# Selective scans: another order of the three VectorE operations of a step, the sliced copy on another engine, and the delta product in four row groups

## The chip, the cores and the metric

The kernel runs on one core of a Trainium2 chip. The metric is the device time of one execution in microseconds (us). Engines are named as the profile names them: PE is TensorE, DVE is VectorE, ACT is ScalarE, POOL is GpSimd, SP is the engine that only issues transfers.

## The reference, cut to what matters

Two layers run on x of shape (4, 64, 64, 128): four images of L = 4096 tokens with 128 channels. Layer 0 is a Mamba block with three scan orders (forward, backward, and "sliced": the tokens taken in 16 interleaved slices). Layer 1 is attention with 16 heads of 8 channels, a small feed-forward part, and a mixture of 64 experts. The change touches layer 0 alone:

```python
xz = in_proj_w @ groupnorm(x)             # 2 * 256 rows: x and z
# for each of three orders:
x = silu(causal_conv1d(x, conv_w, conv_b))          # 4 taps
dt_raw, Bm, Cm = split(x_proj_w @ x, [8, 16, 16])   # along rows
delta = softplus(dt_w @ dt_raw + dt_b)              # 256 rows from 8
A = -exp(A_log)                                     # 256 x 16
def step(h, u_, de_, b_, c_):                       # over 4096 tokens
    dA = exp(de_[..., None] * A)
    h = h * dA + (de_ * u_)[..., None] * b_[:, None, :]
    return h, einsum('bdn,bn->bd', h, c_)
y = (selective_scan(x, delta, A, Bm, Cm) + D * x) * silu(z)
```

The sum of the three orders' y goes through out_proj_w and is added to x.

## The kernel before, in words

Everything is float32. A sequence of 4096 tokens is cut into NC = 4 chunks of T = 1024.

`Inputs` makes what the scans need. `norm` (L251) brings an image, transposes it and normalizes it to the tile xn (128 channels x 4096). `slices` (L301) makes xs, the same tokens in the sliced order, by one GpSimd copy (L305). `of_chunk` makes one chunk of one order: the convolution folded into the input projection (matmuls L361, cv), silu on ACT (L368), the x projection (L375, xd) and its copy to SBUF (L378, xds), whose rows hold B, C and the 8 rows of dt_raw. From these 8 rows the matmuls L394 make the two halves of delta's argument (dt, 2 halves of 256 channels x 2 cuts of 512 tokens). Softplus is made from ACT passes (L399 to L410) and three matmuls a piece that add the parts (L417, sp); VectorE finishes r = delta (L422) and delta * u (L426). delta, du, u, B and C go to DRAM by POOL's queue. The tile pool `ps` has three PSUM tiles.

`Scans.of_image` does an image's scans: 3 orders x 4 chunks x 32 steps = 384 steps. In a step the 128 partitions are 16 channels x 8 states, over 1024 tokens. Its parts:

- `load(s)`, two steps ahead: for every second step delta and du are spread from DRAM over the states (512 KB each), delta by SP's queue, du by SP's, or for image 0 by ACT's; for every fourth step u; at the start of a chunk B and C.
- `exp(s)` (L501), one step ahead on ACT: dA.
- `step(s)` on VectorE: the product du * B (L510), the scan h (L513, tensor_tensor_scan), the product h * C (L515). On GpSimd the last column of h is kept as the start of the next chunk (L514, ends).
- `total(s)` (L521) on TensorE: the sum over the states into one PSUM bank y for a group of four steps. The sums of a group's steps j = 0 and 1 are issued five and four steps later than these, those of j = 2 and 3 four and three steps later.
- `out` (L537) on VectorE: y + D * u, stored by POOL's queue. Then the bank is free.

Buffers: for even steps the product with B goes to a new tile dB (three of them); for odd steps it overwrites du (four). The product with C overwrites the product with B, and the sums L521 read it there. dA has two tiles, delta three, h two.

The order of the work is written out by hand: each part is a generator, and `Pace` advances generators by given shares. There are these stages. The *fill* (to about 2360 us in the profile) advances image 0's scans once for every 1.5 advances of the inputs of all four images, two pieces of inputs at a time. Then `opening(0)` prepares attention for image 0. Then follow four attention loops of 1024 rounds (scores L866, exponentials L871, values L880); beside the first three loops, the scans of the next image advance by a share chosen from how much is left, and what follows attention for the image before (`after`, with matmuls L974 co, L1008 h, L1018 fo and others) is put in between where the one PSUM bank `bank`, which y uses too, is free in the written order. The fourth loop has no scans. The experts end the kernel.

`scan_weights` brings and transposes the weights at the start. In w["x"] the columns for xd are laid out with B at row 0, C at 32 and dt_raw at 64 (72 rows); the dt weights lie in rows 64 to 71 of w["dt"]. Biases, D, taps and A_log come by ACT's queue (A_log half by POOL's).

Of the kernel before, what the change touches and what calls it, by code (L numbers as in the profile page):

```python
# [11 lines left out]
F32 = mybir.dt.float32  # L12
# [4 lines left out]
P = 128  # L17
C = 128
L = 4096
NT = L // P  # L20
DI = 256
NS = 16
R = 8
SLICES = 16
T = 1024
NC = L // T
NS2 = NS // 2
NB = DI // 8
B_ROW, C_ROW, DT_ROW, X_ROWS = 0, 32, 64, 72
H, D, FFN = 16, 8, 512  # L30
VW = 9
VPAD = 168
# [102 lines left out]
def scan_weights(nc, const, load, load_ps, ident, in_proj_w, out_proj_w, dirs):  # L135

    w_z = const["fill"].tile([P, DI], F32, name="w_z")
    w_out = const["all"].tile([P, 2, C], F32, name="w_out")
    w_in = load.tile([P, 4, C], F32, tag="w_in", name="raw_in")
    nc.sync.dma_start(out=w_in, in_=in_proj_w.rearrange("(k p) c -> p k c", p=P))  # L140
    ps = load_ps.tile([P, 512], F32, tag="ps", name="ps_in")
    for m in range(2):
        nc.tensor.transpose(ps[:, m * P : (m + 1) * P], w_in[:, 2 + m, :], ident)
    nc.vector.tensor_copy(w_z, ps[:, :DI])
    raw = load.tile([P, DI], F32, tag="raw", name="raw_out")
    nc.sync.dma_start(out=raw, in_=out_proj_w)
    ps = load_ps.tile([P, 512], F32, tag="ps", name="ps_out")
    for m in range(2):
        nc.tensor.transpose(ps[:, m * P : (m + 1) * P], raw[:, m * P : (m + 1) * P], ident)
    nc.vector.tensor_copy(w_out.rearrange("p m c -> p (m c)"), ps[:, :DI])  # L150
    ws = []
    for i, d in enumerate(dirs):
        w = {}
        raw = load.tile([R + 2 * NS, DI], F32, tag="raw", name=f"raw_x{i}")
        nc.sync.dma_start(out=raw, in_=d["x_proj_w"])
        w["x"] = const["fill"].tile([P, 2, X_ROWS], F32, name=f"w_x{i}")
        nc.gpsimd.memset(w["x"], 0.0)
        for m in range(2):
            ps = load_ps.tile([P, 512], F32, tag="ps", name=f"ps_x{i}_{m}")
            k = R + 2 * NS  # L160
            nc.tensor.transpose(ps[:, :k], raw[:, m * P : (m + 1) * P], ident[:k, :k])
            for row, at, n in ((DT_ROW, 0, R), (B_ROW, R, NS), (C_ROW, R + NS, NS)):
                nc.vector.tensor_copy(w["x"][:, m, row : row + n], ps[:, at : at + n])
        raw = load.tile([P, 2, X_ROWS], F32, tag="raw_dt", name=f"raw_dt{i}")
        nc.gpsimd.memset(raw, 0.0)
        nc.sync.dma_start(out=raw[:, :, DT_ROW:], in_=d["dt_proj_w"].rearrange("(m p) r -> p m r", p=P))
        w["dt"] = const["fill"].tile([X_ROWS, 2, P], F32, name=f"w_dt{i}")
        ps = load_ps.tile([P, 512], F32, tag="ps", name=f"ps_dt{i}")
        for m in range(2):
            nc.tensor.transpose(ps[:X_ROWS, m * P : (m + 1) * P], raw[:, m, :], ident)  # L170
        nc.vector.tensor_copy(w["dt"][DT_ROW:].rearrange("r m p -> r (m p)"), ps[DT_ROW:X_ROWS, :DI])
        for name in ("conv_b", "dt_proj_b"):
            w[name] = const["fill"].tile([P, 2], F32, name=f"{name}{i}")
            nc.scalar.dma_start(out=w[name], in_=d[name].rearrange("(m p) -> p m", p=P))

        w["D"] = const["all"].tile([P, DI // 32], F32, name=f"D{i}")
        for g in range(4):
            nc.scalar.dma_start(out=w["D"][32 * g : 32 * g + 32], in_=d["D"].rearrange("(k p) -> p k", p=32))

        taps = load.tile([P, 2, 4], F32, tag="taps", name=f"taps{i}")  # L180
        nc.scalar.dma_start(out=taps, in_=d["conv_w"].rearrange("(m p) k -> p m k", p=P))
        w["conv"] = const["fill"].tile([P, 4, DI], F32, name=f"conv{i}")
        for k in range(4):
            ps = load_ps.tile([P, 512], F32, tag="ps", name=f"ps_cv{i}_{k}")
            for m in range(2):
                cut = load.tile([P, C], F32, tag="cut", name=f"cut{i}_{k}_{m}")
                nc.vector.tensor_scalar_mul(cut, w_in[:, m, :], taps[:, m, k : k + 1])
                nc.tensor.transpose(ps[:, m * P : (m + 1) * P], cut, ident)
            nc.vector.tensor_copy(w["conv"][:, k, :], ps[:, :DI])
        ws.append(w)  # L190
    for i, (d, w) in enumerate(zip(dirs, ws)):

        w["A"] = const["all"].tile([P, 2, NB // 2], F32, name=f"A{i}")
        a_log = d["A_log"].rearrange("(k d) (q n) -> d q n k", d=16, n=NS2)
        for c in range(16):
            for q, by in enumerate((nc.scalar, nc.gpsimd)):
                by.dma_start(out=w["A"][c * NS2 : (c + 1) * NS2, q, :], in_=a_log[c, q])
    return w_z, w_out, ws


class Inputs:
# [98 lines left out]
    def slices(self, b):  # L300

        nc, xn = self.nc, self.normed[b]
        xs = self.big.tile([P, L + 3], F32, tag="xs", name=f"xs_{b}")
        nc.gpsimd.memset(xs[:, 0:3], 0.0)
        nc.gpsimd.tensor_copy(  # L305
            xs[:, 3:].rearrange("p (j i) -> p j i", i=SLICES),
            xn[:, 3 : L + 3].rearrange("p (i j) -> p j i", i=SLICES),
        )
        self.sliced[b] = xs
        yield  # L310

    def gate(self, b, g):
        nc, xn = self.nc, self.normed[b]
# [17 lines left out]
    def of_chunk(self, b, order, c):  # L331
        while b not in self.normed or (order == 2 and b not in self.sliced):
            yield WAIT
        src = self.sliced[b] if order == 2 else self.normed[b]
        nc, w, key = self.nc, self.ws[order], f"{b}_{order}_{c}"
# [18 lines left out]
        halves = [slice(g * 512, (g + 1) * 512) for g in range(T // 512)]  # L354
        u = self.piece.tile([P, 2, T], F32, tag="u", bufs=2, name=f"u_{key}")
        banks = []
        for m in range(2):
            ps = yield from self.bank(f"cv_{key}_{m}")
# [13 lines left out]
        ps = yield from self.bank(f"xd_{key}")  # L372
# [4 lines left out]
        xd = self.piece.tile([X_ROWS, T], F32, tag="xd", name=f"xds_{key}")  # L377
# [11 lines left out]
        r = self.piece.tile([P, 2, T], F32, tag="r", bufs=2, name=f"r_{key}")  # L389
        banks = []  # L390
        for m in range(2):
            ps = yield from self.bank(f"dt_{key}_{m}")
            for cut in halves:
                nc.tensor.matmul(ps[:, cut], w["dt"][DT_ROW:, m, :], xd[DT_ROW:, cut], start=True, stop=True)  # L394
            banks.append(ps)
        yield
        for m in range(2):
            bias = w["dt_proj_b"][:, m : m + 1]
# [4 lines left out]
        s = self.piece.tile([P, 2, T], F32, tag="s", name=f"s_{key}")  # L403
# [8 lines left out]
        banks = []  # L412
        for m in range(2):
            ps = yield from self.bank(f"sp_{key}_{m}")
# [17 lines left out]
class Scans:  # L432
# [23 lines left out]
    def of_image(self, b, made, alone=False):  # L456

        nc = self.nc
# [3 lines left out]
        steps = [(order, c, k, j) for order in range(3) for c in range(NC) for k in range(8) for j in range(4)]  # L462
        spread, ends, tiles = {}, {}, {}
# [31 lines left out]
        def exp(s):  # L495
            order, c, k, j = steps[s]
            t = tiles["delta", s]
            if j % 2 == 0:
                tiles["delta", s] = self.deep.tile([P, T], F32, tag="dA", bufs=2, name=f"dA_{b}_{s}")
            A = self.ws[order]["A"][:, j % 2, 2 * k + j // 2].unsqueeze(1)  # L500
            nc.scalar.activation(tiles["delta", s], t, AF.Exp, scale=A)  # L501

        def step(s):
            order, c, k, j = steps[s]
            at = 4 * k + j
            dA, du = tiles.pop(("delta", s)), tiles["du", s]
            if j % 2 == 0:
                tiles["du", s] = self.deep.tile([P, T], F32, tag="dB", bufs=3, name=f"dB_{b}_{s}")
            dB = tiles["du", s]
            nc.vector.tensor_mul(dB, du, spread[order, c, "B", j % 2])  # L510
            h = self.deep.tile([P, T], F32, tag="h", bufs=2, name=f"h_{b}_{s}")
            first = 0.0 if c == 0 else ends[order, c - 1][:, at : at + 1]
            nc.vector.tensor_tensor_scan(h, dA, dB, first, ALU.mult, ALU.add)  # L513
            nc.gpsimd.tensor_copy(ends[order, c][:, at : at + 1], h[:, T - 1 :])  # L514
            nc.vector.tensor_mul(dB, h, spread[order, c, "C", j % 2])  # L515

        def total(s, y):
# [37 lines left out]
        n = len(steps)  # L555
# [8 lines left out]
        if b == 0:  # L564
            for w in self.ws:
                nc.scalar.activation(w["A"], w["A"], AF.Exp)
                nc.vector.tensor_scalar_mul(w["A"], w["A"], -1.0)
        exp(0)
        y = None

        def sums(s):
# [913 lines left out]
```

## Time and profile before

| | |
|---|---|
| median of three runs | 13118.68 us (13114.79 to 13125.39) |
| the profiled execution | 13122.38 us, its span 13120.6 us |
| busy in the span | PE 12316.4, DVE 8997.7, ACT 10692.1, POOL 3486.8 us |
| last scan of the fill starts | 2358.3 us |
| L510, L513 and L515 together, all 1536 steps | 1536 of each; about 1.22, 2.29 or 2.35, and 1.23 us of one |

A line of the order of time holds: start in us from the span's start, duration in us, engine, line, operation, out<-in by the program's names with shapes, how many were merged, and in brackets the engine's idle time before it and what ended it, where this is over 0.15 us. In a line of the list of waits stand the engine, its operation and line, what it waited for, the sum in us, how often, and the longest. [...]one operation may start before the end of the one ahead of it on the same engine; starts are the better measure of what an operation costs.

### The profile page before, as it was taken

To read this page: it belongs to the slowest core of one execution; us is meant where nothing else is said; L and a number is where in the kernel's file an instruction comes from. 1 tells how busy PE (TensorE), PEld (TensorE's weight loads), DVE (VectorE), ACT (ScalarE), POOL (GpSimd) and SP (SyncE) were. 2 spreads that over 40 slices of the span, in tenths; PEclk is the share of its full clock that TensorE was granted. 3 is DMA by queue.
4 is the path that set the end of the run, shared out by engine and by line. 5 is a ranking of instruction groups with operands and counts; after the bars stand their busy time and mean duration, and the time that the engine had idled before them with its cause. 6 is when DMAs were issued, how large, how long until landed. Compare 5 with 4: busy or idle time off the path is not lost. (4 is left out here: it accounts for less than half of the span.)

```text
span 13120.6 us, 214395 instructions
## 1 busy us (share of the span) xinstructions
PE 12316.4 (94%) x85447; PEld 3954.2 (30%) x85447; DVE 8997.7 (69%) x8649; ACT 10692.1 (81%) x10789; POOL 3486.8 (27%) x4200
## 2 busy tenths in 40 slices
PE   8898888399999999999999999999999999999995
PEld 3333333122222222233332222333222223333333
DVE  6999999788888877888888778888874211101122
ACT  5666666299999998999999989999998888888871
POOL 2333334222333322233333223333331000000000
PEclk8898888699999999999999999999999999999996
DMA  5666666644444445444444454444443100000004
GB/s 144 192 189 191 195 191 193 173 124 122 123 113 118 113 118 142 125 114 115 114 105 112 121 138 126 112 113 116 109 113 89 55 20 13 22 16 21 13 26 169
DMA packets 686549, 1482.22 MB, mean 113 GB/s; under 512 B 185054, under 2 KB 302374, under 8 KB 685286
## 3 DMA queue, kind: packets, MB, share of 16 engines
q1 hardware_dynamic: 494798, 1049.57, 31.0%
q0 software_dynamic: 139632, 300.84, 7.4%
q10 hardware_dynamic: 51112, 118.08, 3.4%
q8 instruction: 669, 10.96, 0.4%
q14 instruction: 338, 2.77, 0.1%
HBM read 1158.96 MB, written 308.94 MB: 112 GB/s over the span
## 5 line engine op out<-in xcount | busy, mean ns | idle before, releaser
L871 ACT ACTIVATE e<-s 128x1024 f32<-128x1024 f32 x8192 | 7908.9, 1028 | 1117.8 <-PE s L866 905.1
L866 PE MATMUL s<-qm,qT 32*128 32x512 f32 x32768 | 5441.0, 642 | 110.2 <-DMA qT<-d_q 58.9
L880 PE MATMUL acc<-e,v 128*32 128x512 f32 x32768 | 4388.1, 607 | 21.9 <-ACT av L889 19.6
L514 POOL COPY ends<-h 128x1 f32<-128x1 f32 x1536 | 1847.0, 1203 | 4876.5 <-DVE h L513 4869.2
L866 PEld LDWEIGHTS s<-qm,qT 32*128 32x128 f32 x32768 | 1796.7, 183 | 3197.0 <-issue 1416.5
L880 PEld LDWEIGHTS acc<-e,v 128*32 128x32 f32 x32768 | 647.0, 108 | 3160.9 <-issue 3024.1
L513 DVE TENSOR_TENSOR_SCAN h<-dA,ends,dB 128x1024 f32<-128x1024 f32 x576 | 1361.0, 2363 | 184.1 <-ACT dA L501 124.9
L513 DVE TENSOR_TENSOR_SCAN h<-delta,ends,du 128x1024 f32<-128x1024 f32 x576 | 1367.8, 2375 | 160.4 <-ACT delta L501 89.0
L510 DVE TENSOR_TENSOR dB<-du,B 128x1024 f32<-128x1024 f32 x768 | 935.4, 1218 | 190.3 <-PE y L521 182.8
L501 ACT ACTIVATE dA<-delta,A 128x1024 f32<-128x1024 f32 x768 | 888.5, 1157 | 156.9 <-DMA delta<-d_delta 150.8
L501 ACT ACTIVATE delta<-delta,A 128x1024 f32<-128x1024 f32 x768 | 887.8, 1156 | 151.3 <-PE y L521 140.5
L515 DVE TENSOR_TENSOR dB<-h,C 128x1024 f32<-128x1024 f32 x768 | 940.8, 1225 | 26.3
L515 DVE TENSOR_TENSOR du<-h,C 128x1024 f32<-128x1024 f32 x768 | 940.7, 1225 | 26.3
L510 DVE TENSOR_TENSOR du<-du,B 128x1024 f32<-128x1024 f32 x768 | 933.8, 1216 | 0.0
L895 POOL DMA_DIRECT2D d_ctx<-av x512 | 263.8, 524 | 1234.0 <-ACT av L889 1229.1
L361 PE MATMUL cv<-xn,conv 128*128 128x512 f32 x1024 | 511.8, 654 | 21.5 <-DVE xn L297 18.3
L521 PE MATMUL y<-du,sel 128*32 128x256 f32 x6144 | 492.5, 393 | 8.7 <-DVE du L515 8.7
L521 PE MATMUL y<-dB,sel 128*32 128x256 f32 x6144 | 497.3, 397 | 2.5 <-DVE dB L515 2.5
L513 DVE TENSOR_TENSOR_SCAN h<-dA,dB 128x1024 f32<-128x1024 f32 x192 | 446.9, 2328 | 52.7 <-ACT dA L501 32.6
L513 DVE TENSOR_TENSOR_SCAN h<-delta,du 128x1024 f32<-128x1024 f32 x192 | 440.1, 2292 | 38.4 <-ACT delta L501 14.4
L537 DVE SCALAR_TENSOR_TENSOR o<-us,D,y 128x256 f32<-128x256 f32 x384 | 205.9, 536 | 354.9 <-PE y L521 343.3
L550 POOL DMA_DIRECT2D d_y<-o x512 | 328.5, 669 | 276.3 <-DVE o L537 255.5
(252 smaller groups left out, 7609.2 us busy)
## 6 DMA issues: line engine op xcount, KB each, us to landing
delta<-d_delta SPq DMA_DIRECT2D x768, 512.0 KB
du<-d_du SPq DMA_DIRECT2D x576, 512.0 KB
du<-d_du ACTq DMA_DIRECT2D x192, 512.0 KB
d_u<-u POOLq DMA_DIRECT2D x48, 1024.0 KB, 5.6
B<-d_bc SPq DMA_DIRECT2D x96, 512.0 KB
C<-d_bc SPq DMA_DIRECT2D x96, 512.0 KB
d_delta<-r POOLq DMA_DIRECT2D x48, 1024.0 KB, 4.9
d_du<-u POOLq DMA_DIRECT2D x48, 1024.0 KB, 6.1
```

The costliest lines, as they stand in the source:

```text
L361: nc.tensor.matmul(ps[:, cut], w["conv"][:, k, m * P : (m + 1) * P], reads(k, g), start=(k == 0), stop=(k == 3))
L501: nc.scalar.activation(tiles["delta", s], t, AF.Exp, scale=A)
L510: nc.vector.tensor_mul(dB, du, spread[order, c, "B", j % 2])
L513: nc.vector.tensor_tensor_scan(h, dA, dB, first, ALU.mult, ALU.add)
L514: nc.gpsimd.tensor_copy(ends[order, c][:, at : at + 1], h[:, T - 1 :])
L515: nc.vector.tensor_mul(dB, h, spread[order, c, "C", j % 2])
L521: nc.tensor.matmul(y[32 * g : 32 * g + 32, : T // 4], self.sel[:, j // 2, :], hC[:, 256 * g : 256 * g + 256], start=(j == 0), stop=(j == 3),)
L550: nc.gpsimd.dma_start(out=to.rearrange("p (i j) -> p i j", i=SLICES)[:, :, at : at + n], in_=rows.rearrange("p (i j) -> p i j", i=SLICES),)
L866: nc.tensor.matmul(s_ps[:, k, :], qT[at : at + 32, kc * P : (kc + 1) * P], queries[j, qb][at : at + 32, :], start=True, stop=True,)
L871: nc.scalar.activation(e, s_ps, AF.Exp, scale=1.0 / math.sqrt(D))
L880: nc.tensor.matmul(accs[j, qb][32 * k : 32 * k + 32, :], v[:, kc, h * VW : h * VW + 32], es[i][k // 2][:, k % 2, :], start=(kc == 0), stop ...
L895: nc.gpsimd.dma_start(out=self.context[b][h * D : h * D + D, cut], in_=av[32 * k : 32 * k + D, :])
```

## The change

1. In `of_image` the product with B becomes a function of its own, `inputs(s)`. It runs once before the first step; after that `step(s)` calls `inputs(s + 1)` between its scan and its product with C. So the order on VectorE is: scan s, product with B of s + 1, product with C of s, scan s + 1. The tile dB is taken accordingly earlier.
2. The last column of h is kept only for the first three chunks of an order, as nothing reads that of the fourth.
3. `slices` makes xs by four ACT copies of 128x1024 instead of one GpSimd copy of 128x4096, with a yield after each.
4. In w["x"] the eight columns of dt_raw are repeated at rows 0, 32, 64 and 96 (B goes to row 8, C to 40; 104 rows in all), and the dt weights likewise, by four transfers an order instead of one, two each on SP's and ACT's queues. The four matmuls of delta (2 halves x 2 cuts) each read another of these four groups of rows, and are issued one after the other once both PSUM tiles are there.

On TensorE and ACT the order of all else stays the same, except that around the sliced copies a few pieces move by a place or two; there are as many matmuls as before.

```diff
-B_ROW, C_ROW, DT_ROW, X_ROWS = 0, 32, 64, 72
+B_ROW, C_ROW, X_ROWS = 8, 40, 104
...
-            for row, at, n in ((DT_ROW, 0, R), (B_ROW, R, NS), (C_ROW, R + NS, NS)):
+            for row, at, n in [(32 * g, 0, R) for g in range(4)] + [(B_ROW, R, NS), (C_ROW, R + NS, NS)]:
                 nc.vector.tensor_copy(w["x"][:, m, row : row + n], ps[:, at : at + n])
...
-        nc.sync.dma_start(out=raw[:, :, DT_ROW:], in_=d["dt_proj_w"].rearrange("(m p) r -> p m r", p=P))
+        for g in range(4):
+            by = (nc.sync, nc.scalar)[g % 2]
+            by.dma_start(out=raw[:, :, 32 * g : 32 * g + R], in_=d["dt_proj_w"].rearrange("(m p) r -> p m r", p=P))
...
-        nc.vector.tensor_copy(w["dt"][DT_ROW:].rearrange("r m p -> r (m p)"), ps[DT_ROW:X_ROWS, :DI])
+        nc.vector.tensor_copy(w["dt"].rearrange("r m p -> r (m p)"), ps[:X_ROWS, :DI])
...
-        nc.gpsimd.tensor_copy(
-            xs[:, 3:].rearrange("p (j i) -> p j i", i=SLICES),
-            xn[:, 3 : L + 3].rearrange("p (i j) -> p j i", i=SLICES),
-        )
+        to = xs[:, 3:].rearrange("p (j i) -> p j i", i=SLICES)
+        src = xn[:, 3 : L + 3].rearrange("p (i j) -> p j i", i=SLICES)
+        n = L // SLICES // NC
+        for g in range(NC):
+            nc.scalar.copy(to[:, g * n : (g + 1) * n, :], src[:, g * n : (g + 1) * n, :])
+            yield
         self.sliced[b] = xs
-        yield
...
         for m in range(2):
-            ps = yield from self.bank(f"dt_{key}_{m}")
-            for cut in halves:
-                nc.tensor.matmul(ps[:, cut], w["dt"][DT_ROW:, m, :], xd[DT_ROW:, cut], start=True, stop=True)
-            banks.append(ps)
+            banks.append((yield from self.bank(f"dt_{key}_{m}")))
+        for m in range(2):
+            for g, cut in enumerate(halves):
+                at = 32 * (2 * m + g)
+                rows = slice(at, at + R)
+                nc.tensor.matmul(banks[m][:, cut], w["dt"][rows, m, :], xd[rows, cut], start=True, stop=True)
...
+        def inputs(s):
+            order, c, k, j = steps[s]
+            du = tiles["du", s]
+            if j % 2 == 0:
+                tiles["du", s] = self.deep.tile([P, T], F32, tag="dB", bufs=3, name=f"dB_{b}_{s}")
+            nc.vector.tensor_mul(tiles["du", s], du, spread[order, c, "B", j % 2])
+
         def step(s):
+
             order, c, k, j = steps[s]
             at = 4 * k + j
-            dA, du = tiles.pop(("delta", s)), tiles["du", s]
-            if j % 2 == 0:
-                tiles["du", s] = self.deep.tile([P, T], F32, tag="dB", bufs=3, name=f"dB_{b}_{s}")
-            dB = tiles["du", s]
-            nc.vector.tensor_mul(dB, du, spread[order, c, "B", j % 2])
+            dA, dB = tiles.pop(("delta", s)), tiles["du", s]
             h = self.deep.tile([P, T], F32, tag="h", bufs=2, name=f"h_{b}_{s}")
             first = 0.0 if c == 0 else ends[order, c - 1][:, at : at + 1]
             nc.vector.tensor_tensor_scan(h, dA, dB, first, ALU.mult, ALU.add)
-            nc.gpsimd.tensor_copy(ends[order, c][:, at : at + 1], h[:, T - 1 :])
+            if c < NC - 1:
+                nc.gpsimd.tensor_copy(ends[order, c][:, at : at + 1], h[:, T - 1 :])
+            if s + 1 < n:
+                inputs(s + 1)
             nc.vector.tensor_mul(dB, h, spread[order, c, "C", j % 2])
...
         exp(0)
+        inputs(0)
```

## The prediction

> **What bounds the kernel now.** I read the page's slices first, because an average hides the stages.
>
> ```profile
> span 13120.6 us, 214395 instructions
> ...
> PE   8898888399999999999999999999999999999995
> ...
> DVE  6999999788888877888888778888874211101122
> ACT  5666666299999998999999989999998888888871
> ```
>
> There are two regimes. In slices 1 to 7 (up to about 2360 us) VectorE is at 9 and TensorE at 8; from slice 9 on TensorE stays at 9. The chain of waits goes back only to 9955 us and is nearly all L866 and L880 (TensorE), so it says nothing of the first regime. Busy time by stretch does (columns: PE, PEld, DVE, ACT, POOL busy with counts, clock, DMA share, GB/s):
>
> ```profile
> 140.00:2362.00 2222.00, 1932.15 (x6627) 768.40 (x6631) 2110.70 (x1450) 1463.21 (x1173) 818.11 (x938) 0.88 0.66 192
> 2700.00:4500.00 1800.00, 1795.94 (x14148) 514.16 (x14144) 1552.76 (x1062) 1706.92 (x1790) 587.03 (x672) 1.00 0.48 118
> ```
>
> The first row is the fill: the 384 scan steps of image 0 beside the inputs of all images. VectorE is idle 111 us of 2222, and its waits for others in that stretch add up to 49 us (29 for exponentials, 6 for L417, 5 for the sums L521, the rest norms). The other 62 us are its own gaps. So here VectorE sets the pace. The second row is an attention loop: TensorE is busy 99.8%, and VectorE's 14% of idle time costs nothing. Which gaps are its own, the order of time on VectorE in the fill shows:
>
> ```profile
> 1001.94 1.22 DVE L510 TENSOR_TENSOR dB<-du,B 128x1024 f32<-128x1024 f32 x1
> 1003.29 2.29 DVE L513 TENSOR_TENSOR_SCAN h<-dA,dB 128x1024 f32<-128x1024 f32 x1
> 1005.62 1.23 DVE L515 TENSOR_TENSOR dB<-h,C 128x1024 f32<-128x1024 f32 x1
> 1006.76 2.35 DVE L422 TENSOR_TENSOR r<-r,sp 128x1024 f32<-128x1024 f32 x2
> ```
>
> From start to start: product with B to its scan 1.35, scan to its product with C 2.33, but that product to the next, which does not need it, 1.14, with the same duration of 1.22 to 1.23. What an operation costs when its reader does not come next is seen at the end of the fill, where strangers fall between:
>
> ```profile
> 2346.36 1.22 DVE L510 TENSOR_TENSOR du<-du,B 128x1024 f32<-128x1024 f32 x1
> 2347.49 0.28 DVE L659 COPY w_comb<-ps_comb 128x128 f32<-128x128 f32 x1
> 2347.71 2.35 DVE L513 TENSOR_TENSOR_SCAN h<-delta,ends,du 128x1024 f32<-128x1024 f32 x1
> 2349.98 0.65 DVE L665 COPY w<-ps_w 8x512 f32<-8x512 f32 x1
> 2350.56 1.20 DVE L515 TENSOR_TENSOR du<-h,C 128x1024 f32<-128x1024 f32 x1
> ```
>
> A stranger starts 1.13 after the product and 2.27 after the scan; the 0.28 copy is free, as the scan still comes 1.35 after its product. Last, the sliced copy on GpSimd:
>
> ```profile
> 965.53 8.20 POOL L305 COPY xs<-xn 128x4096 f32<-128x4096 f32 x1
> 966.78 9.11 DVE L513 TENSOR_TENSOR_SCAN h<-dA,dB 128x1024 f32<-128x1024 f32 x1
> ```
>
> A scan that takes 2.29 elsewhere takes 9.11 here, and all four copies meet one such scan (9.21, 9.11, 9.13, 9.16). It is counted as busy, so no list of waits shows it.
>
> **What the Trainium skill says.** "VectorE: DVE Perf Modes", section "The DRAIN you can't avoid", says that the next operation cannot start until the pipe is empty and that a semaphore between operations costs nothing extra. The trace differs: 1.35 with the dependence, 1.14 without. "SBUF — State Buffer", section "SBUF: two separate sides", says that VectorE with two SBUF inputs and a GpSimd operation that reads SBUF exclude each other for a whole instruction; the 9.11 us scan agrees. "TensorEngine Tiling (Array Packing)", section "Tiling Modes": "Tiles operate independently". The scores L866, in four row groups, agree: at 11100.47 us four start within 0.02 and the next four 0.53 later.
>
> **The change, part by part.**
>
> *Product a step ahead.* The order becomes scan s, product with B of s+1, product with C of s, scan s+1. No operation follows its source. A step with a carry (L513 with ends) now takes 1.35 + 2.385 + 1.14 = 4.88; then 2.27 + 1.14 + 1.14 = 4.55. Without the carry, 4.82 becomes 2.21 + 1.14 + 1.14 = 4.49 (2.21 is what the equally long 2.29 us L426 takes before a stranger). That is 0.33 a step, 0.325 by medians: 384 × 0.325 = **-125 us** in the fill. The sources are old enough: h is ready 2.39 after the scan's start and read at 3.41.
>
> *The wait it moves.* The even product writes a new dB tile of three, freed by the sums L521 of six steps before. For j = 2 these sums are issued in the very step before, and the product now stands ahead of the product with C. Paired over the fill, the sums ended before the new place in 79 of 93 such steps; in 14 they ended later, 23 us in all. Behind the waiting product stand the product with C (its sums come 13 us later in the median) and the next scan. I add that and a little for faster VectorE meeting bursts of TensorE and ScalarE: **+25 us**, bounds 5 and 65. Loads are needed only 1.14 us earlier; du was waited for once, at the start.
>
> *Sliced copy to ScalarE.* Four scans lose the excess over 2.29 or 2.35: 6.86 + 6.82 + 6.78 + 6.81 = **-27 us**. ScalarE gets 16 copies of 128x1024. No row has this strided read there: 1.0 each as the contiguous L272, 2.05 if a quarter of GpSimd's 8.2; 16 to 33 us. I take 1.2, hidden in 759 us of ScalarE's idle time; the exponential ends 9.8 us ahead of its scan in the median in the fill. Without that cover a copy costs its length, 33 at most, which the 65 above holds. The first reader L361, which waited 43.5 us for L305, gains.
>
> *Four row groups for delta.* Eight L394 matmuls take 3.67 in a row; as two sets of four, about 1.1 to 1.3. 48 × 2.5 = 120 us off TensorE in the fill, which is not the bound: 0 by itself, but it shortens the ScalarE chain (L399 waited 153.5 us for L394) by about what VectorE gains in a chunk (9.6 steps × 0.325 = 3.1), so the feeds keep up. This is why I add only 25 above.
>
> *Start.* Six more loads on ScalarE's queue (0.4 to 0.5 each) stand ahead of its first copy at 45.9, three more on SP's queue, and 18 copies of 128x8 on VectorE, which is idle there. +3, up to +8; the first chunk's delta (6.16 us on a slow clock) gives 2.5 back: **0**. GpSimd loses 384 of its 1536 end copies: 0, it is 37% busy.
>
> *Loops.* 1152 steps also get shorter, but TensorE is the bound: 0. The moved wait there falls on almost every second even step (164 to 171 us an image on VectorE), inside its idle time. Near 5300 to 5450 and 7800 to 8050 VectorE is busy 92 to 93% and TensorE loses 26 us; some is won, and the opening of image 0 gains 12 × 0.33. Against that, o (L537) comes one product later and holds the one PSUM bank. Net **-4**, from -15 to +15.
>
> Sum: -125 + 25 - 27 + 0 - 4 = -131. Against the profiled execution, 13122.4 (span 13120.6 and 1.8 around it), 12991; the median of the runs is 3.7 lower: **12988 us**.
>
> **Rivals.**
> *Feeds become the bound.* TensorE was busy 87% of the fill, and exponentials were only just in time at 5% of the scans. If half the gain of 152 turns into such waits: about 13050. For it: bursts. Against it: the 120 us taken off TensorE.
> *The change does not do it.* If the order costs the same whatever the dependence, as the skill's section has it, only the copy gains: 13118.7 - 27 = 13092. Against it: the strangers above.
> *Slower: o behind the waiting product.* In the attention loops the product for j = 2 waits for TensorE, the product with C and the scan follow later, then o, for whose bank a matmul of L974 or L1008 waits. Such a first user follows o 140 times in images 2 and 3, in the median 3.7 us after it, in one case of ten at once. To cancel the gain TensorE must lose 131 / 140 = 0.94 us at every one; beyond that it is slower, at 2 us 13119 - 131 + 280 = 13268. Against it: three quarters have over 2 us, and the delay is about one product, 1.14.
>
> **How the numbers follow.** Main case 68%, from 12955 (no new waits, seams -15, start +3) to 13025; feeds 20%, 13025 to 13075; no effect of order 6%, 13075 to 13110; slower 4%, and 2% for what I have not seen. A measurement of this kernel can tell about 0.2%, 26 us, so faster means under 13092. The range of 12955 to 13055 holds the main case and most of the second. Faster: 68 + 20 + half of 6 and some = 92%; same 4%; slower 4%.
>
> **What would show it.** Scan to the next product 2.21 or 2.27, then 1.14 and 1.14; no scan above 2.4; eight L394 matmuls in about 1.2; the fill's last scan near 2235 instead of 2358; the loops as long as before. The forecast is wrong if VectorE's waits in the fill rise far above 75 us, or if TensorE shows new waits for L537's successor in the loops.

## The result, and the profile after

The changed kernel takes 13003.85 us in the median (12998.01 to 13010.74), against 13118.03 us (13114.79 to 13125.39) for the kernel before, measured beside it: a ratio of 0.9912, interval 0.9895 to 0.993. That is 114 us less, where 130 were forecast. The profiled execution's span fell from 13120.6 to 12995.9 us, by 10 us more than the medians: that of the changed kernel is its fastest run, that of the kernel before (13122.38 us) lies above its median. The stages below account for these two executions.

The slices of the page of the changed kernel:

```profile
span 12995.9 us, 213975 instructions
...
PE   7788887399999999999999999999999999999995
DVE  6999999788888777888887778888874211101122
ACT  5676766399999988999999889999998888888881
```

The two regimes are still there: VectorE at 9 in slices 2 to 7, TensorE at 9 after slice 8. By stage of the profiled executions:

| us | before | after | difference |
|---|---|---|---|
| start of the span to the first scan | 138.1 | 135.2 | -2.9 |
| fill, first to last scan of image 0 | 2220.2 | 2127.9 | -92.3 |
| opening of attention | 245.9 | 247.6 | +1.7 |
| attention loops with scans (1, 2, 3) | 2552.2, 2607.6, 2591.0 | 2555.9, 2591.2, 2580.1 | +3.7, -16.4, -10.9 |
| attention loop without scans (4) | 2472.8 | 2467.0 | -5.8 |
| end | 292.8 | 290.9 | -1.9 |

Busy time by stretch in the changed kernel, in the columns of the same view of before (stretch, length, then PE, PEld, DVE, ACT, POOL with counts, clock, DMA share, GB/s):

```profile
140.00:2267.00 2127.00, 1787.85 (x6625) 713.20 (x6629) 2009.22 (x1441) 1487.32 (x1189) 688.38 (x833) 0.89 0.68 200
2700.00:4500.00 1800.00, 1795.93 (x14140) 514.25 (x14140) 1499.14 (x1055) 1706.03 (x1789) 429.33 (x603) 1.00 0.48 118
```

Against the first row of the same view of before, which is 95 us longer, VectorE's busy time fell by 101.5 us (2110.70 to 2009.22), but its idle time rose from 111 to 118 us. TensorE's busy time fell by 144 us. In the loop of the second row TensorE stays at 99.8%.

VectorE in the order of time, in the fill of the changed kernel (start, duration, engine, line; the product with B is now L513, the scan L522, the product with C L527):

```profile
999.38 2.28 DVE L522 TENSOR_TENSOR_SCAN h<-dA,dB 128x1024 f32<-128x1024 f32 x1
1001.58 1.20 DVE L513 TENSOR_TENSOR du<-du,B 128x1024 f32<-128x1024 f32 x1
1002.69 1.22 DVE L527 TENSOR_TENSOR dB<-h,C 128x1024 f32<-128x1024 f32 x1
1003.83 2.29 DVE L522 TENSOR_TENSOR_SCAN h<-delta,du 128x1024 f32<-128x1024 f32 x1
```

Start to start: 2.20, 1.11, 1.14. Medians over the fill for a step with a carry: 2.262 + 1.117 + 1.135 = 4.51 us, before 2.385 + 1.351 + 1.143 = 4.88. Each operation now starts before the end of the one ahead, while before, the product with B and the scan had each ended before their reader started. No scan of the fill takes over 2.5 us; four took 9.1 to 9.2 before.

But VectorE now waits more for others. Its largest waits in the fill (engine, operation, line, what it waited for: sum in us, times, longest), first in the kernel before, then in the changed kernel:

```profile
DVE h L513 <- ACT dA L501: 17.7, 10, 3.2
DVE h L513 <- ACT delta L501: 11.5, 7, 2.9
DVE dB L510 <- PE y L521: 5.4, 6, 1.3
```

```profile
DVE h L522 <- ACT dA L506: 37.3, 24, 4.9
DVE dB L513 <- PE y L533: 21.9, 13, 3.9
DVE h L522 <- issue: 21.1, 8, 4.2
DVE h L522 <- ACT delta L506: 21.0, 14, 5.0
```

Together with the smaller ones this is 115 us, where it was 49. The first and fourth lines are scans that wait for their exponential (L506, on ScalarE): 58 us instead of 29. In the third line, "issue", the profile names nothing that was waited for; but each of these eight scans starts 0.09 us after the end of its exponential, as the scans of the first and fourth lines do, so they are most likely the same wait: 79 us in all. The exponential still ends well ahead of its scan in the median (8.0 us, before 9.8), but the lead that the shortest tenth does not exceed shrank from 1.8 to 0.09 us. The second line is the moved wait: the product with B for the sums (L533) that free its dB tile.

The sum for the fill closes when the times from start to start, without the waits, are added over all steps. The products with B fell from 513.2 to 428.2 us, the scans from 934.9 to 862.1, and the products with C stayed (438.4 and 438.5): 158 off. Of these 27 belong to the four long scans and 130 to the order, 0.34 a step. (384 times the 0.365 of the medians would be 140. That is too much, as an operation that a wait follows costs its whole duration: 1.22 instead of 1.14 us for a product with C, 37 times instead of 7.) 66 came back as waits, and all other operations took 1 less: 92 off, as measured.

### The profile page after: what moved, and what is told of

Same layout as the page of the kernel before. It is cut to its first block, busy times and chain, and to the rows that moved or that the text cites. A ratio compares the mean times of both kernels' runs of the same rounds, so it can differ in the third digit from the quotient of the medians.

```text
span 12995.9 us, 213975 instructions
## 1 busy us (share of the span) xinstructions
PE 12144.6 (93%) x85447; PEld 3889.7 (30%) x85447; DVE 8718.8 (67%) x8667; ACT 10713.5 (82%) x10805; POOL 2923.0 (22%) x3812
## 5 line engine op out<-in xcount | busy, mean ns | idle before, releaser
L524 POOL COPY ends<-h 128x1 f32<-128x1 f32 x1152 | 1267.1, 1101 | 3356.0 <-DVE h L522 3337.5
L522 DVE TENSOR_TENSOR_SCAN h<-delta,ends,du 128x1024 f32<-128x1024 f32 x576 | 1351.2, 2346 | 215.9 <-ACT delta L506 185.2
L522 DVE TENSOR_TENSOR_SCAN h<-dA,ends,dB 128x1024 f32<-128x1024 f32 x576 | 1350.9, 2345 | 148.4 <-ACT dA L506 144.9
L513 DVE TENSOR_TENSOR dB<-du,B 128x1024 f32<-128x1024 f32 x768 | 928.2, 1209 | 627.8 <-PE y L533 603.0
L506 ACT ACTIVATE delta<-delta,A 128x1024 f32<-128x1024 f32 x768 | 887.2, 1155 | 151.1 <-PE y L533 142.1
L506 ACT ACTIVATE dA<-delta,A 128x1024 f32<-128x1024 f32 x768 | 887.9, 1156 | 140.1 <-DMA delta<-d_delta 105.2
L527 DVE TENSOR_TENSOR du<-h,C 128x1024 f32<-128x1024 f32 x768 | 935.7, 1218 | 0.1
L527 DVE TENSOR_TENSOR dB<-h,C 128x1024 f32<-128x1024 f32 x768 | 935.6, 1218 | 0.0
L513 DVE TENSOR_TENSOR du<-du,B 128x1024 f32<-128x1024 f32 x768 | 921.2, 1200 | 0.0
L364 PE MATMUL cv<-xn,conv 128*128 128x512 f32 x1024 | 498.7, 640 | 25.4 <-DVE xn L299 17.3
L562 POOL DMA_DIRECT2D d_y<-o x512 | 328.4, 669 | 793.6 <-DVE o L549 728.9
L533 PE MATMUL y<-du,sel 128*32 128x256 f32 x6144 | 487.5, 390 | 12.6 <-DVE du L527 12.6
L533 PE MATMUL y<-dB,sel 128*32 128x256 f32 x6144 | 490.4, 392 | 3.4 <-DVE dB L527 3.4
L522 DVE TENSOR_TENSOR_SCAN h<-delta,du 128x1024 f32<-128x1024 f32 x192 | 438.6, 2284 | 52.1 <-ACT delta L506 45.7
L522 DVE TENSOR_TENSOR_SCAN h<-dA,dB 128x1024 f32<-128x1024 f32 x192 | 438.5, 2284 | 40.4 <-ACT dA L506 38.7
L558 POOL DMA_DIRECT2D d_y<-o x512 | 254.3, 503 | 674.7 <-DVE o L549 663.4
```

The source lines that it names most:

```text
L364: nc.tensor.matmul(ps[:, cut], w["conv"][:, k, m * P : (m + 1) * P], reads(k, g), start=(k == 0), stop=(k == 3))
L513: nc.vector.tensor_mul(tiles["du", s], du, spread[order, c, "B", j % 2])
L533: nc.tensor.matmul(y[32 * g : 32 * g + 32, : T // 4], self.sel[:, j // 2, :], hC[:, 256 * g : 256 * g + 256], start=(j == 0), stop=(j == 3),)
L562: nc.gpsimd.dma_start(out=to.rearrange("p (i j) -> p i j", i=SLICES)[:, :, at : at + n], in_=rows.rearrange("p (i j) -> p i j", i=SLICES),)
```

## The experiments

Each kernel's times stand beside runs of the kernel before on the same chip; "fill" is the time from the first to the last scan of image 0 in its profile (2220.2 before, 2127.9 after), "waits" the sum of VectorE's waits over 0.15 us in it (49 and 115). Each fill and each sum of waits is that of one profiled execution. How well two of them agree can be seen where two kernels do the same: over the 45 steps before the first sliced copy, the changed kernel and the one with the copy on GpSimd stay within 0.4 us of each other. The kernels were timed on several occasions; where the intervals of two ratios overlap, a difference in time is not settled. No kernel leaves anything out.

### Each part alone

**The new order alone.** The kernel before with the product a step ahead, and nothing else:

```diff
...
+        def inputs(s):
+            order, c, k, j = steps[s]
+            du = tiles["du", s]
+            if j % 2 == 0:
+                tiles["du", s] = self.deep.tile([P, T], F32, tag="dB", bufs=3, name=f"dB_{b}_{s}")
+            nc.vector.tensor_mul(tiles["du", s], du, spread[order, c, "B", j % 2])
...
+            if s + 1 < n:
+                inputs(s + 1)
             nc.vector.tensor_mul(dB, h, spread[order, c, "C", j % 2])
...
+        inputs(0)
```

> The kernel before with the new order of the three VectorE operations alone (no other part of the change). Theory A (dependent neighbours on VectorE cost, and VectorE sets the fill): the fill from first to last scan of image 0 was 2220 us; 384 steps lose 0.365 each, 140 us, and waits grow as they did in the changed kernel, by about 65: fill near 2145, time near 13020. The four scans beside the sliced copy stay at 9.2 us. Rival B (the feeds of ScalarE and TensorE bound the fill as soon as VectorE is faster, and only the row groups for delta relieve them): fill not under 2180, time 13055 or more.

Measured: 13029.75 us (13027.22 to 13044.91), ratio 0.9934 (0.9919 to 0.9949): 89 us of the 114. Fill 2160.9 (-59), waits 121: nearer to theory A than to the rival. Added from start to start, the order is worth 131 us of VectorE's time here too, and 72 come back as waits. All end copies are kept here, so leaving out those of the fourth chunk is not what shortened the steps. The loops with scans take 2556.1, 2594.4 and 2580.4, as in the changed kernel: their gain belongs to the order.

**The sliced copy on ScalarE alone.**

```diff
-        nc.gpsimd.tensor_copy(... xs ..., ... xn ...)
...
+        for g in range(NC):
+            nc.scalar.copy(to[:, g * n : (g + 1) * n, :], src[:, g * n : (g + 1) * n, :])
+            yield
```

> The kernel before with the sliced copy on ScalarE alone. Theory A (the GpSimd copy held VectorE's scan, four times 6.8 us): no scan of the fill over 2.4 us, fill shorter by 20 to 27, time 13091 to 13098. Rival B (the long scan was time that VectorE would have waited for its feeds anyway): the four scans are short but VectorE's waits grow by as much, fill within 5 us of before.

Measured: 13113.03 us (13104 to 13119), ratio 0.9994 (0.9986 to 1.0003): no difference that can be told. The long scans are gone and VectorE's busy time from the first to the last scan is 27 us less (2108.9 before, 2081.4 here), but the fill is only 6 us shorter (2214.2): waits rose from 49 to 72, those of scans for exponentials from 29 to 45. That is close to what the rival said.

**The row groups alone.**

```diff
...
+        for m in range(2):
+            for g, cut in enumerate(halves):
+                at = 32 * (2 * m + g)
+                rows = slice(at, at + R)
+                nc.tensor.matmul(banks[m][:, cut], w["dt"][rows, m, :], xd[rows, cut], start=True, stop=True)
```

> The kernel before with the four row groups for delta alone. Theory A: TensorE is relieved by 120 us in the fill and is not the bound, so the fill changes by at most the part of VectorE's 49 us of waits that hangs on L394's chain: 0 to -15, time 13103 to 13118. Rival B (the feeds are at the bound already): fill shorter by more than 25.

Measured: 13106.74 us (13097 to 13119), ratio 0.9990 (0.9984 to 0.9997). Fill 2205.3 (-15), waits 35 instead of 49. So a change on TensorE, which is not the pacing engine here, still gains: VectorE waits less for what TensorE and ScalarE feed it.

**The change without its row groups**, that is, the order and the copy together (the diff just shown, reversed; the end copies of the fourth chunk stay left out).

> The changed kernel without the row groups for delta (new order, sliced copy on ScalarE). Theory A with its estimate that the row groups keep the feeds in step: VectorE's waits in the fill rise from 115 to about 140, fill near 2153 instead of 2128, time near 13030. Rival B (feeds are the bound of the changed fill): waits above 180, fill over 2190, time over 13065. If the row groups do nothing: fill 2128 and time 13004.

Measured: 13037.17 us (13033.51 to 13047.97), ratio 0.9940 (0.9923 to 0.9956). Its waits of VectorE in the fill, in the columns used above:

```profile
DVE dB L509 <- PE y L529: 54.3, 23, 4.4
DVE h L518 <- ACT dA L502: 39.3, 25, 4.9
DVE h L518 <- issue: 27.1, 9, 4.5
DVE h L518 <- ACT delta L502: 22.1, 13, 3.4
```

Waits add up to 160 us and the fill takes 2172.9, 12 more than with the order alone: with the feeds behind, moving the copy to ScalarE made the fill longer instead of 27 shorter. (The times of these two kernels, 13037.17 and 13029.75, have overlapping intervals.) The result lies between the two theories, nearer to A. The row groups that are missing here are worth 45 us of fill and 33 us of time, three times what they bring alone. Eight of these matmuls in one row, in the kernel before and then with row groups in the changed kernel (start, duration, engine, line):

```profile
1008.12 3.67 PE L394 MATMUL dt<-xds,w_dt 8*128 8x512 f32 x8 [1.15 <-DVE r L422]
```

```profile
1059.49 1.14 PE L400 MATMUL dt<-xds,w_dt 8*128 8x512 f32 x8
```

The change's gain is thus not a sum of three gains made apart. Alone, by fill: 59 + 6 + 15 = 80; together 92. Order and row groups without the copy's move give all of it, as the next run shows.

### The copy's place

**The copy back on GpSimd**, with order and row groups kept:

```diff
-        for g in range(NC):
-            nc.scalar.copy(to[:, g * n : (g + 1) * n, :], src[:, g * n : (g + 1) * n, :])
-            yield
...
+        nc.gpsimd.tensor_copy(... xs ..., ... xn ...)
```

> The changed kernel with the sliced copy back on GpSimd, as one copy of 128x4096 (new order and row groups stay; ends are kept for all four chunks, as before). Four scans are long again, 27 us on VectorE; ScalarE has 31.5 us less. Theory A (most of the 27 is given back, as the pause lets the feeds catch up and ScalarE is spared): fill 2128 to 2143, time 13004 to 13019. Rival B (the 27 us count in full): fill 2155, time 13031.

Measured: 12997.63 us (12994.15 to 12999.75), ratio 0.9905 (0.9891 to 0.992), fill 2122.9, waits 84: not slower than the changed kernel, and better than both theories had it. The expectation says that end copies are kept for all four chunks; this kernel leaves out those of the fourth, as the changed kernel does. Its copies do hold VectorE, as before: two scans take 9.36 and 9.34 us, two products with B 8.18 and 8.23. VectorE in the order of time, in this kernel:

```profile
1472.58 2.34 DVE L521 TENSOR_TENSOR_SCAN h<-dA,ends,dB 128x1024 f32<-128x1024 f32 x1
1474.84 8.23 DVE L512 TENSOR_TENSOR du<-du,B 128x1024 f32<-128x1024 f32 x1
1482.99 1.21 DVE L526 TENSOR_TENSOR dB<-h,C 128x1024 f32<-128x1024 f32 x1
```

A product of 1.20 us takes 8.23 and the next start is 8.15 later. The four hold VectorE for 28 us too long (9.36 + 9.34 - 2 × 2.34 + 8.18 + 8.23 - 2 × 1.20), and its waits for others are 31 us fewer than in the changed kernel (84 against 115). What the lock costs, the waits give back, and they do so right behind each copy: step by step, this kernel falls about 7 us behind the changed one at each copy, and within some 20 steps most of it is regained. Two things can give it back: the pause, in which TensorE and ScalarE work ahead, and ScalarE's time, as this kernel lacks the four copies (7.9 us) that the changed kernel has on ScalarE at the same place. This run does not part the two.

**The copies on ScalarE made twice**, to price ScalarE's time:

```diff
-            nc.scalar.copy(to[:, g * n : (g + 1) * n, :], src[:, g * n : (g + 1) * n, :])
+            for _ in range(2):
+                nc.scalar.copy(to[:, g * n : (g + 1) * n, :], src[:, g * n : (g + 1) * n, :])
```

> The changed kernel with each of the 16 sliced copies on ScalarE made twice: 31.5 us more on ScalarE (1.97 each), nothing else. Theory A (in the changed fill ScalarE's in-order queue is what VectorE's waits come from): the fill grows by 10 to 30 us, time 13014 to 13034. Rival B (ScalarE has 640 us of idle time in the fill, and the waits come from TensorE): 0 to 5.

Measured: 13018.07 us (13015.3 to 13020.9), ratio 0.9922 (0.9905 to 0.9939); fill 2140.0, waits 128. So 31.5 us more on ScalarE, idle for 30% of the fill, cost 12 us of fill, as theory A said, and 14 us of time (the intervals overlap). The copies themselves in the changed kernel (the tile's view: least, middle and longest in ns, first and last start in us):

```profile
L311 ACT COPY xs<-xn x16: 1953/1969/2001, 367.5 to 2043.4; 128x1024 f32<-128x1024 f32 x16
```

They take 1.97 us each, near the upper bound of the prediction and not at the 1.2 it took.

**The copies on VectorE itself**, 16 pieces of 1.05 us:

```diff
-            nc.scalar.copy(to[:, g * n : (g + 1) * n, :], src[:, g * n : (g + 1) * n, :])
+            nc.vector.tensor_copy(to[:, g * n : (g + 1) * n, :], src[:, g * n : (g + 1) * n, :])
```

> The changed kernel with the 16 sliced copies on VectorE. ScalarE has 31.5 us less; VectorE gets 16 copies of 128x1024, 0.7 us each if as quick as the normalizing L299, 1.14 if as a product: 11 to 18 us. Theory A (ScalarE's time costs 12 us of fill for 31.5, VectorE's counts in full): the fill changes by 0 to +6. Rival B (waits are where VectorE's own time vanishes): the fill is shorter by about 12.

Measured: 12995.73 us (12989.06 to 13000.26), ratio 0.9904 (0.9887 to 0.992); fill 2120.0, waits 94. Work of 16.8 us put on the pacing engine did not lengthen the fill; its waits fell by 21 instead, which is nearer to the rival. All three places of the copy have overlapping intervals.

### What the new waits are made of

Two theories could explain the 115 us. One: each wait has a cause of its own (a tile too few, a load in a bad place on a queue, too much work on ScalarE), and to remove it shortens the fill. The other: TensorE, ScalarE and VectorE feed each other in a ring (VectorE's r, L427, frees the PSUM tiles in which TensorE starts the next dt, L400, and cv, L364; ScalarE makes u and softplus's parts from these, and the exponentials between them), and to remove one wait only moves it to another.

**A fourth dB tile**, so that no product with B waits for sums (x_g and o get one tile less to make room):

```diff
...
-                tiles["du", s] = self.deep.tile([P, T], F32, tag="dB", bufs=3, name=f"dB_{b}_{s}")
+                tiles["du", s] = self.deep.tile([P, T], F32, tag="dB", bufs=4, name=f"dB_{b}_{s}")
...
```

> The changed kernel with four tiles dB instead of three (room from x_g and o with one tile less each). VectorE's 22 us of waits for the sums at the product with B in the fill should go, and those in the loops, 603 us over all in the page, too. Theory A (VectorE sets the fill): fill shorter by 10 to 22, loops unchanged, time 12982 to 12994. Rival B (the next wait, for the exponential, takes their place): fill shorter by less than 5, time 13000 to 13008.

Measured: 13007.32 us (13004.87 to 13009.17), ratio 0.9913 (0.9898 to 0.9928); fill 2130.7, waits 119. VectorE's largest waits in the fill:

```profile
DVE h L522 <- ACT dA L506: 43.7, 28, 4.9
DVE h L522 <- ACT delta L506: 24.9, 16, 5.0
DVE h L522 <- issue: 21.9, 8, 4.3
```

The wait of 21.9 us for the sums is gone, and 10 us of it turn up in the waits for exponentials, 8 in the norm's statistics (8.7 us instead of 0.4, waiting for the transposed image on ScalarE), the rest in other lines. The 8 may come from the smaller x_g; this run does not part the two. The rival was right. In the loops, too, the 581 us that the product with B waited for sums are gone and scans wait 407 us more for exponentials (763 instead of 356); as TensorE is the bound there, VectorE's idle time could only change its name, and the three loops together take 7724 us instead of 7727.

**The du loads of image 0 on SP's queue** instead of ScalarE's:

```diff
-                by = nc.scalar if alone and name == "du" else nc.sync
+                by = nc.sync
```

> The changed kernel with the du loads of image 0 issued by SP's queue instead of ScalarE's. On ScalarE they wait for the sums L533 of eight steps before (142 us in 30 waits) with exponentials queued behind. Theory A: ScalarE gets further ahead, VectorE's waits in the fill fall from 115 to about 85, time near 12975. Rival B (these waits come when ScalarE is far ahead anyway; and SP's queue now holds delta loads behind du): no change or slower, 13004 to 13030.

Measured: 13007.42 us (13002.98 to 13011.02), ratio 0.9913 (0.9898 to 0.9928); fill 2142.6, waits 130. ScalarE's waits in the fill, first in the changed kernel, then in this one:

```profile
ACT xds L381 <- PE xd L378: 156.8, 46, 6.2
ACT delta L506 <- PE y L533: 142.1, 30, 17.9
ACT u L371 <- PE cv L364: 127.9, 35, 8.6
```

```profile
ACT u L371 <- PE cv L364: 212.2, 49, 13.5
ACT xds L381 <- PE xd L378: 174.9, 45, 6.5
```

ScalarE's 142 us of waiting for the sums (it issues the du loads, whose tiles the sums free) vanish, its waits for the convolution grow by 84, and the fill is longer by 15. Of these 6 come from its earlier start (first scan at 129.1 instead of 135.2). In time the two kernels cannot be told apart. This is what the rival said, which named another reason too: on SP's queue delta loads now stand behind those of du.

**Both silus of a gate together**, which saves 20 loads of activation tables on ScalarE:

```diff
...
-            nc.scalar.activation(s_g[:, m, :], ps, AF.Silu)
...
+        for m in range(2):
+            nc.scalar.activation(s_g[:, m, :], banks[m], AF.Silu)
```

> The changed kernel with both silu passes of a gate one after the other (two PSUM tiles held together), so that ScalarE changes its function tables about 20 times less in the fill, 1.28 us each: 26 us less on ScalarE. Theory A (waits for exponentials come from ScalarE's queue; doubling its copies, 31.5 us more, cost 12 us of fill): fill shorter by about 10, time near 12993. Rival B (TensorE holds the feeds): no change, or longer, as two PSUM tiles of three are held at once.

Measured: 12999.33 us (12993.65 to 13006.46), ratio 0.9908 (0.9893 to 0.9922); ScalarE's busy time in the fill fell by 30 us (1476 to 1446 between 140 and 2240 us), and the fill is 2129.3, waits 116. Scans wait 9 us less for exponentials or their issue, products with B 9 us more for sums. So 31.5 us more on ScalarE cost 12, and 30 us less gain nothing that can be told, though here two of the three PSUM tiles are held at once, which may cost something itself. As far as these runs go, ScalarE's time is a limit only beyond what the others allow.

These three runs fit the ring better than the single causes. They do not prove it, as each of them carries a second change (less room for x_g and o, delta loads behind du, PSUM tiles held together). Which member of the ring is the last one stays open: no run here took time from all three at once.

### Two combinations

Gate silus together and the copies on VectorE:

> The changed kernel with both: gate's silus together and the sliced copies on VectorE. Sum of the two by theory A: fill shorter by 4 to 10, time 12994 to 13000.

12986.65 us (12985.3 to 12996.47), ratio 0.9899 (0.9885 to 0.9914); fill 2123.2, waits 97. This is the fastest kernel here, faster than its sum had it. All its four runs lie below all four of the changed kernel (by 17 us in the medians), but the two intervals overlap and the two were timed on different occasions, so I call this likely and not settled.

Gate silus together and the copy on GpSimd:

> New order and row groups with the sliced copy on GpSimd as before and gate's silus together. The sliced copy on GpSimd gave 12998 and a fill of 2123. Theory A: ScalarE has 58 us less than in the changed kernel; fill 2108 to 2118, time 12983 to 12993, the fastest of all.

12993.5 us (12985.74 to 13002.62), ratio 0.9903 (0.9888 to 0.9918); fill 2124.1, waits 85. The fill is not shorter than with the copy on GpSimd alone (2122.9), nor is this the fastest of all, as the expectation had it: putting the silus together gained nothing here either.

## Why the prediction was right, and where its steps were off

The forecast of 12988 us, the range and the sign held: 13003.85 lies 16 us above the forecast and inside the main case (12955 to 13025). The total came out close because errors of its terms cancelled: the waits were 41 us larger than forecast, the gains of order and loops 25 larger. That part is luck.

- **The product a step ahead (-125): right, in mechanism and nearly in size.** Added over all steps it gave 130 us of VectorE's time. The strangers that the profile of before showed were a sound model: 1.117 where 1.143 was assumed from the product with B to its follower, 2.262 where 2.27 was from the scan. The Trainium skill's "VectorE: DVE Perf Modes", section "The DRAIN you can't avoid", says besides what the prediction took from it: "A next op that is not held starts earlier". The strangers fit that sentence, so the section is less at odds with the trace than the prediction had it. It gives no size for a neighbour that reads the result; by these medians such a neighbour costs 0.12 us more after a scan and 0.23 more after a product.
- **The moved wait and the feeds (+25): sized too small.** It measured +66, just past the upper bound of 65. The wait for dB itself was well paired: 23 us forecast, 21.9 found for the product with B, where 5 stood before. The rest of the term, "a little" for a faster VectorE that meets bursts, was 50 more for exponentials, if those named as issue are counted with them. The sum judged the feeds by the median lead of the exponentials, 9.8 us, and left the scans whose exponential was only just in time (5% of them, which it had counted) to a rival; it is these short leads that a faster VectorE uses up. After the change 15% of the scans start within 0.3 us of their exponential's end.
- **The sliced copy (-27): this step failed.** The long scans did vanish, but with order and row groups kept, the copy's move gained nothing (12997.63 with the copy on GpSimd, 13003.85 without). Alone it gained 6 us of fill; without the row groups it lost 12. The prediction counted a blocked scan as time on the path. The runs show that the waits behind it grow by nearly as much when it goes; that this is because TensorE and ScalarE get ahead in a pause of 7 us is argued, as the copies on ScalarE stand at the same place. And the copy came to ScalarE at 31.5 us, not 19, hidden only in part: doubling it cost 12. As to the lock, "SBUF — State Buffer", section "SBUF: two separate sides", of the Trainium skill agrees a second time: beside GpSimd's copy a product of 1.20 us takes 8.23.
- **Four row groups (0 by itself): wrong as a sum, right as an argument.** Eight matmuls take 1.14 as estimated. The text said that they keep the feeds in step, then priced them at nothing. Alone they give 15 us of fill, in the full change 45. Their share stood hidden in the small +25. The 9.6 steps a chunk of its argument should be 8 (384 steps over 48 chunks), so that VectorE gains 2.6 us a chunk where the row groups take 2.5 off TensorE.
- **Start (0):** -2.9 us. **Loops (-4):** -23.6 in the three loops with scans, below the bound of -15. The opening's gain of 12 × 0.33 did not come (+1.7). The new order alone shows the same loops. TensorE's waits for the output o, in loop 2 of the kernel before and then of the changed kernel:

```profile
PE co L974 <- DVE o L537: 9.8, 5, 2.6
PE xT L1039 <- DVE o L537: 5.4, 1, 5.4
PE h L1008 <- DVE o L537: 3.2, 4, 1.4
```

```profile
PE xT L1052 <- DVE o L549: 4.7, 1, 4.7
PE co L987 <- DVE o L549: 3.6, 3, 1.6
PE h L1021 <- DVE o L549: 0.6, 1, 0.6
```

  The sums fell from 18.4 to 8.9 us, and from 21.3 to 13.2 in loop 3. That is 18 of the 27 us that the two loops gained; the rest stands as less busy time of TensorE (7.5 and 4.3 us), for which no run gives a cause. Loop 4 has no scans and was 6 us shorter in this profile; among all kernels it takes from 2466 to 2473, which I cannot explain.
- **The rivals.** "Feeds become the bound" forecast half of 152 turned into waits, 13050. Of the 158 us that order and long scans brought, 66 returned as waits, two fifths: the mechanism is at work, somewhat weaker than the rival had it. "The change does not do it" is refuted by the starts. "Slower: o behind the waiting product": the product with B does wait more for sums in the loops (581 us instead of 177 over loops 1 to 3), but this lies inside VectorE's idle time, and TensorE waits for o less, not more.

Among the tests the prediction set, the starts, the long scans and the eight matmuls came out as written. The last scan of the fill starts at 2263.2, not near 2235, and the waits of 115 us, far above 75, are the sign that it had named for its own failure: the main case held on the time, but the feeds had entered it.

## What to carry to other kernels

An order of dependent operations on VectorE can be priced from the profile of before: look where a stranger stands after the same operation, take starts and not durations, and multiply; check the product afterwards by a sum over all steps, as medians overstated it by 10 us in 140 here. Time in which an engine is held by a lock is not all gain when removed: here most or all of it came back as waits for the engines that feed it, so price the feeds by their shortest leads, not by the median. A relief for engines that are not the bound belongs in the sum of the change that makes the bounding engine faster.

## What was not expected of the hardware

- A copy of 128x1024 float32 whose source has a step of 256 elements (1 KB) takes 1.97 us on ScalarE and 1.05 on VectorE. (ScalarE's contiguous copy of that size, L272, which takes 1.01, reads PSUM, so it does not show what the step alone costs.) The strided copy of four times as much takes 8.2 on GpSimd.
- GpSimd's copy held both kinds of VectorE operation with two SBUF inputs that it met, a product (8.23 us instead of 1.20) as well as a scan (9.34 instead of 2.34), and the profile counts the time as VectorE's busy time.
- Eight float32 matmuls with 8 rows of contraction and 512 columns, in one row without a wait between them, take 3.67 us in one row group and 1.14 in four.
